# Averages of squares as a 128 by 112 block in a hybrid vision network on one core

## The chip, the cores and the metric

The kernel runs on one core of a Trainium2 chip. The metric is the device time of one execution in microseconds; lower is better. The time before is the median of three runs.

## The reference

Four layers work on an image batch of 4 x 56 x 56 pixels with 96 channels, in fp32. Layer 0 is a vision state-space block: normalization over channels, a projection, four selective scans over the 3136 pixels of an image (rows, rows reversed, columns, columns reversed) with 192 channels and 16 states each, a gated output projection, and a feed-forward part. Layer 1 is another block of that kind with a convolution branch; its scan output is normalized over 192 channels, and its fused output over 96. Layers 2 and 3 are linear attention (no softmax) and a feed-forward part with 8-bit and 16-bit rounding, each behind a normalization.

What the change touches is the normalization, which occurs all over the network:

```python
def _ln(x, g, b, eps=1e-05):
    m = x.mean(-1, keepdims=True)
    v = x.var(-1, keepdims=True)
    return (x - m) * jax.lax.rsqrt(v + eps) * g + b

def _ln_t(v, eps=1e-5):
    m = jnp.mean(v, axis=-1, keepdims=True)
    s = jnp.var(v, axis=-1, keepdims=True)
    return (v - m) / jnp.sqrt(s + eps)
```

## The kernel before, in words

Channels lie on partitions, pixels along the free dimension. An image's 3136 pixels are cut into 7 chunks of 448 (`CW`, `CS`), and a chunk into four blocks of 112 (`NT`).

**The scans.** 2 layers x 4 images x 4 directions x 7 chunks x 2 halves of the channels x 4 groups of states make 1792 rounds. In each round VectorE forms two products of 448 columns (L719) and runs three scans (L726), ScalarE forms three decays (L678) straight into PSUM banks, GpSimd forms the third product (L714) and the multiplication by C (L768), and TensorE spreads B over partitions (L616, bank `b`) and sums over the states into `y` (L799): four products with 32-column weights, each into its own 32 output partitions. Chunk by chunk TensorE also forms the parameters of later chunks (L448, L496).

**The fillers.** All other work on images is put between these steps as "lanes": Python generators that run in chunks (`load`, `middle`, `branch`, `fuse`, `attend`). The order on TensorE, ScalarE, VectorE and GpSimd is the order in which the program issues instructions. Each `yield` of a generator names the slot in which its next step may be issued (C or F, two slots a round), the number of PSUM banks that it will hold, and its declared cost on ScalarE (a) and TensorE (p). In the scans at most 3 chunks are alive (`DEPTH`) and 2 banks are held (`BANKS`); `room` and `spend` keep the declared backlogs below 4.0 and 7.0. The zeros: at most rounds `keep_busy` (L778) issues products with a weight of zeros ahead of the next spread of B, so that TensorE stays busy. Their number is a constant less 1.6 for each unit of p declared since the last time:

```python
self.add_zeros(int(max(0.0, WARM - self.work) + 0.5))   # WARM = 6.8
self.work += PER_P * pe                                 # PER_P = 1.6, in spend
```

**The tail.** When the last scan has ended, `late` widens the limits: 6 chunks alive, 4 banks held, and a ring of all eight PSUM banks (`self.ring`). What is left of `fuse` and `attend` of the last image then runs without the planner's limits on declared costs.

**The normalization.** `factor` (L820) centres a chunk on TensorE, `squares` (L836) squares it on ScalarE, and `spread_factor` (L841) averages the squares over channels, takes the power -0.5, and gives a factor for each pixel and channel by which VectorE multiplies (L889, L1211, L1251; `fuse` first copies the factor of its 192 channels at L1197). `spread_factor` has three ways:

- at the start, before the scans (`self.tables` is false): products with the squares as weights and one column of averages as moving side give a block of 112 pixels by 4; ScalarE adds eps (L864), GpSimd takes the power (L865), and four products spread it (L875);
- in the scans: the same block of 112 by 4 (L860), then Ln and Exp on ScalarE (L870, L871), and four products whose weights are a repeated column of `rs` and whose moving side is the identity (L875);
- in the tail (`self.ring`): one product of the 96 by 96 averages with the squares gives 96 by 448 (L850), and Ln and Exp (L852, L853) on that whole block write over the squares, so nothing has to be spread.

Of the kernel before, what the change touches and what calls it, by code (L numbers as in the profile page):

```python
# [11 lines left out]
F32 = mybir.dt.float32  # L12
# [3 lines left out]
AF = mybir.ActivationFunctionType  # L16
ALU = mybir.AluOpType
# [5 lines left out]
C = 96  # L23
# [5 lines left out]
NT = 112  # L29
CW = 448  # L30
# [137 lines left out]
class Net:  # L168
# [672 lines left out]
    def spread_factor(self, eps, *terms):  # L841

        nc = self.nc
        if self.ring:
            ps, f = self.ps()[:C, :CW], terms[0][0][:C]
            for n, (sq, avg) in enumerate(terms):
                nc.tensor.matmul(ps, avg, sq, start=n == 0, stop=n == len(terms) - 1)  # L850
            yield "F1 a1.2"
            nc.scalar.activation(f, ps, AF.Ln, bias=self.eps[eps][:C])  # L852
            nc.scalar.activation(f, f, AF.Exp, scale=-0.5)  # L853
            yield "C0"
            return f
        ps = self.ps()
        blocks = [slice(q * NT, (q + 1) * NT) for q in range(4)]
        for q, b in enumerate(blocks):
            for n, (sq, avg) in enumerate(terms):
                nc.tensor.matmul(ps[:NT, q : q + 1], sq[:, b], avg[:, :1], start=n == 0, stop=n == len(terms) - 1)  # L860
        rs = self.wp.tile([NT, 4], F32, name="rs", bufs=12)
        if not self.tables:
            yield "F0 a.3"
            nc.scalar.activation(rs, ps[:NT, :4], AF.Identity, bias=self.eps[eps][:NT])  # L864
            nc.gpsimd.tensor_tensor(rs, rs, self.power[:NT], ALU.pow)  # L865
            yield "C1 p2.4"
        else:

            yield "F1 a.6"
            nc.scalar.activation(rs, ps[:NT, :4], AF.Ln, bias=self.eps[eps][:NT])  # L870
            nc.scalar.activation(rs, rs, AF.Exp, scale=-0.5)  # L871
            yield "C1 p2.4"
        ps = self.ps()[:C, :CW]
        for q, b in enumerate(blocks):
            nc.tensor.matmul(  # L875
                ps[:, b], rs[:, q : q + 1].to_broadcast([NT, C]), self.ident[:NT, :NT], start=True, stop=True
            )
        return ps
# [553 lines left out]
```

## Time and profile before

| | |
|---|---|
| median of three runs | 8124.83 us (8120.56 to 8125.09) |
| the profiled execution, its own time | 8113.91 us |
| its span, first to last instruction | 8112.0 us |
| mean granted TensorE clock | 0.898 of full speed |
| start, before the scans run steadily | to about 122 us |
| scans with fillers | about 122 to 7897 us |
| tail | about 7897 to 8112 us |
| calls of `spread_factor`: start, scans, tail | 5, 213, 34 |

How to read it: PE is TensorE, PEld its weight loads, DVE VectorE, ACT ScalarE, POOL GpSimd, SP the engine that issues the DMAs here. A line of a group or list names the source line, the engine, the operation and the tiles (out<-in). In a list of waits, "DVE h L719 <- PE b L616" means that VectorE's L719 waited until TensorE's L616 was done, followed by the total in us, the times, and the longest. An fp32 matmul counts as two instructions. Busy ends of TensorE are modelled, so distances between starts say more than durations.

### The profile page before, as it was taken

To read this page: it belongs to the slowest core of one execution; us is meant where nothing else is said; L and a number is where in the kernel's file an instruction comes from. 1 tells how busy PE (TensorE), PEld (TensorE's weight loads), DVE (VectorE), ACT (ScalarE), POOL (GpSimd) and SP (SyncE) were. 2 spreads that over 40 slices of the span, in tenths; PEclk is the share of its full clock that TensorE was granted. 3 is DMA by queue.
4 is the path that set the end of the run, shared out by engine and by line. 5 is a ranking of instruction groups with operands and counts; after the bars stand their busy time and mean duration, and the time that the engine had idled before them with its cause. 6 is when DMAs were issued, how large, how long until landed. Compare 5 with 4: busy or idle time off the path is not lost.

```text
span 8112.0 us, 112271 instructions
## 1 busy us (share of the span) xinstructions
PE 7168.4 (88%) x33189; PEld 2503.7 (31%) x33189; DVE 7522.7 (93%) x9600; ACT 6094.8 (75%) x12759; POOL 7167.9 (88%) x3989
## 2 busy tenths in 40 slices
PE   7889888889888988889889889998899988999887
PEld 3233233222332223322232223333233322433233
DVE  6999999999999999999999999999989999899982
ACT  6778878786778767886677866787767877678776
POOL 5999999999999999999989998899988999789980
PEclk8889989899998988999889998889988898898987
DMA  5555665567556666566555665555655556555552
GB/s 177 180 185 188 198 193 183 174 198 222 182 179 193 208 196 188 178 201 193 189 180 180 197 220 176 174 162 169 195 178 164 168 174 195 167 164 166 173 163 66
DMA packets 568235, 1467.46 MB, mean 181 GB/s; under 512 B 108034, under 2 KB 337156, under 8 KB 566756
## 3 DMA queue, kind: packets, MB, share of 16 engines
q1 hardware_dynamic: 566848, 1458.49, 57.3%
q8 instruction: 261, 4.28, 0.2%
q14 instruction: 354, 2.90, 0.1%
q10 hardware_dynamic: 772, 1.80, 0.1%
HBM read 1186.49 MB, written 273.47 MB: 180 GB/s over the span
## 4 chain that ended last, share of the span: by engine, by line
PE 34%; DVE 30%; ACT 16%; issue 12%; POOL 4%; DMA 2%; SPq 0%; DVEq 0%; POOLq 0%; ACTq 0%
DVE h L726 22%; PE y L799 7%; DVE h L719 7%; PE y L786 5%; ACT da L678 5%; PE y L795 4%; PE b L616 3%; POOL hc L768 2%; PE pp L496 2%; ACT L830 2%; PE pp L448 2%; PE ps L875 1%; PE ps L947 1%; PE ps L860 1%; ACT Y L806 1%
## 5 line engine op out<-in xcount | busy, mean ns | idle before, releaser
L726 DVE TENSOR_TENSOR_SCAN h<-da,h 128x449 f32<-128x449 f32 (+1 forms) x5376 | 5505.1, 1071 | 101.0 <-ACT da L678 84.0
L768 POOL TENSOR_TENSOR hc<-h,cb 128x1344 f32<-128x1344 f32 x1792 | 4883.1, 2725 | 615.1 <-DVE h L726 490.0
L678 ACT ACTIVATE da<-dt,na 128x448 f32<-128x448 f32 x5376 | 3353.6, 632 | 1109.4 <-DVE h L726 1087.3
L719 DVE TENSOR_TENSOR h<-du,b 128x448 f32<-128x448 f32 x3584 | 2015.8, 603 | 132.5 <-PE b L616 86.3
L799 PE MATMUL y<-hc,four 128*32 128x448 f32 x14336 | 1918.2, 610 | 18.8 <-POOL hc L768 18.5
L714 POOL TENSOR_TENSOR h<-du,cb 128x448 f32<-128x448 f32 x1792 | 1753.5, 979 | 54.4 <-ACT h L691 29.8
L786 PE MATMUL y<-w,zeros 128*96 128x448 bf16 x5067 | 1415.0, 398 | 0.0
L616 PE MATMUL b<-cf,sel 128*128 128x448 bf16 x1792 | 679.1, 379 | 667.5 <-DVE h L719 661.1
L786 PEld LDWEIGHTS <-zeros 128*96 128x96 bf16 x5067 | 629.3, 135 | 1168.5 <-issue 1011.7
L448 PE MATMUL pp<-U,wd 96*128 96x448 f32 x896 | 666.6, 833 | 14.2 <-DMA U<-u 4.5
L799 PEld LDWEIGHTS y<-hc,four 128*32 128x32 f32 x14336 | 294.8, 113 | 1198.6 <-issue 681.3
L795 PE MATMUL y<-Y,ident 96*96 96x448 f32 x672 | 542.1, 896 | 37.8 <-ACT Y L806 19.8
L496 PE MATMUL pp<-cf,wd 12*96 12x448 f32 (+1 forms) x896 | 484.8, 623 | 89.9 <-ACT dtc L506 55.8
L521 POOL TENSOR_TENSOR duc<-dtc,U 96x896 f32<-96x896 f32 x224 | 482.9, 2156 | 34.6 <-ACT dtc L508 34.6
L696 ACT COPY carry<-h 128x3 f32<-128x3 f32 x1536 | 302.0, 197 | 260.6 <-DVE h L726 254.6
L806 ACT COPY Y<-y 96x448 f32<-96x448 f32 x448 | 342.1, 764 | 29.7 <-PE y L799 28.5
L691 ACT COPY h<-carry 128x3 f32<-128x3 f32 x1536 | 280.0, 182 | 51.3 <-POOL hc L768 48.4
L587 ACT COPY cf<-pp 64x448 f32<-64x448 f32 x448 | 235.6, 526 | 81.0 <-PE pp L609 72.7
L506 ACT ACTIVATE dtc<-pp,wd 96x448 f32<-96x448 f32 x448 | 281.6, 629 | 18.5 <-PE pp L496 14.0
L616 PEld LDWEIGHTS <-sel 128*128 128x128 bf16 x1792 | 184.9, 103 | 349.2 <-issue 280.7
L860 PEld LDWEIGHTS ps<-avg,w 96*112 96x112 f32 (+2 forms) x1936 | 246.2, 191 | 94.7 <-issue 58.4
L875 PEld LDWEIGHTS ps<-ident,rs 112*96 112x96 f32 x1744 | 217.3, 187 | 131.4 <-issue 89.4
(381 smaller groups left out, 5597.3 us busy)
## 6 DMA issues: line engine op xcount, KB each, us to landing
cb<-cd SPq DMA_DIRECT2D x896, 448.0 KB, 4.8
dt<-dd SPq DMA_DIRECT2D x448, 672.0 KB, 5.6
du<-dd SPq DMA_DIRECT2D x448, 672.0 KB, 5.8
dd<-dtc SPq DMA_DIRECT2D x672, 112.0 KB, 2.0
dd<-duc SPq DMA_DIRECT2D x672, 112.0 KB, 2.0
win<-m SPq DMA_DIRECT2D x252, 112.0 KB, 4.4
U<-u SPq DMA_DIRECT2D x112, 168.0 KB, 4.6
w<-z SPq DMA_DIRECT2D x84, 224.0 KB, 4.3
```

What stands on the lines that cost most here:

```text
L448: self.nc.tensor.matmul(ch.ps.rearrange("p (a b) -> p a b", b=HS), ch.par.wx[:, e], self.in_order(self.U[e], ch.orient, ch.c * CS, CS), st ...
L496: self.nc.tensor.matmul(ch.pd, ch.par.wt[rows, C * e : C * e + C], ch.cf[rows], start=True, stop=True)
L521: self.nc.gpsimd.tensor_tensor(in_rows(ch.duc), in_rows(ch.dtc), u[:, :, lo : lo + CS // HS], ALU.mult)
L616: self.nc.tensor.matmul(ps, self.sel[:, q], self.upper(ch.cf), start=True, stop=True)
L678: nc.scalar.activation(da[g][:, INNER], ch.dt[e][:, g], AF.Exp, scale=ch.par.na[:, e, q, g : g + 1])
L714: nc.gpsimd.tensor_tensor(tokens(hs[n])[:, 2], ch.du[e][:, 2], ch.cb[q][:, 1], ALU.mult)
L719: nc.vector.tensor_tensor(tokens(hs[n])[:, g], ch.du[e][:, g], bs[n], ALU.mult)
L726: nc.vector.tensor_tensor_scan(h[:, way], da[g][:, way], h[:, way], 0.0, ALU.mult, ALU.add)
L768: nc.gpsimd.tensor_tensor(hc, tokens(hs[n]), ch.cb[q][:, 0].unsqueeze(1).to_broadcast([128, NG, CS]), ALU.mult,)
L786: self.nc.tensor.matmul(self.y[:C], self.zeros[:, :C], self.some, start=False, stop=False)
L795: nc.tensor.matmul(o, w, self.in_order(a, ch.orient, ch.c * CS, CS), start=True, stop=False)
L799: nc.tensor.matmul(self.y[32 * n : 32 * n + 32], self.four, hc[:, g], start=n == 3, stop=n == 3 or q == NQ - 1,)
```

## The change

In the scans and in the tail, `spread_factor` averages the squares by four products with 32 columns of averages as weights (`avg[:, :32]`) and a block of 112 pixels as the moving side. Each product writes its own 32 partitions, so the result is a block of 128 partitions by 112, in which each 32 partitions repeat one block's averages. For two terms (in `fuse`) the four products of the second term follow those of the first. Ln and Exp act on this 128 by 112 block into a new tile `rsb` with 4 buffers. Four more products spread it: the weights are an identity column (0, 32, 64 or 96) repeated over 96 columns, the moving side is `rsb`. The declared cost of this last step is p1.4, where the old spread declared p2.4. The tail loses its own way: its factor now lies in a PSUM bank, and the step after Exp holds a bank and goes through TensorE. The way of the start stays, with 3 buffers of `rs` in place of 12.

```diff
         nc = self.nc
-        if self.ring:
-            ps, f = self.ps()[:C, :CW], terms[0][0][:C]
-            for n, (sq, avg) in enumerate(terms):
-                nc.tensor.matmul(ps, avg, sq, start=n == 0, stop=n == len(terms) - 1)
-            yield "F1 a1.2"
-            nc.scalar.activation(f, ps, AF.Ln, bias=self.eps[eps][:C])
-            nc.scalar.activation(f, f, AF.Exp, scale=-0.5)
-            yield "C0"
-            return f
         ps = self.ps()
         blocks = [slice(q * NT, (q + 1) * NT) for q in range(4)]
+        if self.tables:
+            for n, (sq, avg) in enumerate(terms):
+                for q, b in enumerate(blocks):
+                    nc.tensor.matmul(
+                        ps[32 * q : 32 * q + 32, :NT], avg[:, :32], sq[:, b], start=n == 0, stop=n == len(terms) - 1
+                    )
+            rs = self.wp.tile([128, NT], F32, name="rsb", bufs=4)
+            yield "F1 a.6"
+            nc.scalar.activation(rs, ps[:, :NT], AF.Ln, bias=self.eps[eps])
+            nc.scalar.activation(rs, rs, AF.Exp, scale=-0.5)
+            yield "C1 p1.4"
+            ps = self.ps()[:C, :CW]
+            for q, b in enumerate(blocks):
+                row = self.ident[:, 32 * q : 32 * q + 1].to_broadcast([128, C])
+                nc.tensor.matmul(ps[:, b], row, rs, start=True, stop=True)
+            return ps
         for q, b in enumerate(blocks):
             for n, (sq, avg) in enumerate(terms):
                 nc.tensor.matmul(ps[:NT, q : q + 1], sq[:, b], avg[:, :1], start=n == 0, stop=n == len(terms) - 1)
-        rs = self.wp.tile([NT, 4], F32, name="rs", bufs=12)
-        if not self.tables:
-            yield "F0 a.3"
-            nc.scalar.activation(rs, ps[:NT, :4], AF.Identity, bias=self.eps[eps][:NT])
-            nc.gpsimd.tensor_tensor(rs, rs, self.power[:NT], ALU.pow)
-            yield "C1 p2.4"
-        else:
-
-            yield "F1 a.6"
-            nc.scalar.activation(rs, ps[:NT, :4], AF.Ln, bias=self.eps[eps][:NT])
-            nc.scalar.activation(rs, rs, AF.Exp, scale=-0.5)
-            yield "C1 p2.4"
+        rs = self.wp.tile([NT, 4], F32, name="rs", bufs=3)
+        yield "F0 a.3"
+        nc.scalar.activation(rs, ps[:NT, :4], AF.Identity, bias=self.eps[eps][:NT])
+        nc.gpsimd.tensor_tensor(rs, rs, self.power[:NT], ALU.pow)
+        yield "C1 p2.4"
         ps = self.ps()[:C, :CW]
         for q, b in enumerate(blocks):
             nc.tensor.matmul(
```

## The prediction

> **What bounds the kernel now.** I read the page from the top: span and engine shares, then VectorE's and TensorE's lists of waits inside the scan stage (122 to 7897 us, some 96% of the span), then one averaging step in the timeline of TensorE, then the busy time in stretches of the tail.
>
> The engine shares (busy us, share of the span, instructions) come first.
>
> ```profile
> span 8112.0 us, 112271 instructions
> PE   7168.4 (88%) x33189; PEld 2503.7 (31%) x33189; DVE 7522.7 (93%) x9600; ACT 6094.8 (75%) x12759; POOL 7167.9 (88%) x3989
> ```
>
> VectorE is the busiest. From 122 to 7897 us it works 7410.4 of 7775 us, so only 365 us (4.7%) of the scan stage are open to any gain at all, unless VectorE's own work shrinks, and the change doesn't shrink it. What ends its idle time there (us in total, times, longest):
>
> ```profile
> DVE h L726 <- ACT da L678: 81.4, 165, 2.5
> DVE h L719 <- PE b L616: 76.7, 93, 2.9
> DVE w L889 <- PE ps L875: 33.5, 19, 3.7
> ...
> DVE xra L889 <- PE ps L875: 10.3, 10, 2.7
> ...
> DVE xq L1251 <- PE ps L875: 7.3, 4, 4.2
> ...
> DVE w L1211 <- PE ps L875: 3.6, 4, 2.0
> ```
>
> Two kinds of TensorE lateness touch the change: the spread of B (L616) comes late 93 times in 1792 rounds, and the spread factor (L875) 37 times, 54.7 us together. TensorE itself mostly waits for VectorE:
>
> ```profile
> PE b L616 <- DVE h L719: 654.1, 713, 2.8
> ```
>
> So TensorE has slack in most rounds and is late in a few crowded ones. An averaging step, as TensorE runs it (start, duration, instructions):
>
> ```profile
> 4011.96 0.86 PE L860 MATMUL ps<-avg,w 96*112 96x1 f32 x8
> 4012.68 0.36 PE L616 MATMUL b<-cf,sel 128*128 128x448 bf16 x1
> 4012.97 0.96 PE L799 MATMUL y<-hc,four 128*32 128x448 f32 x8
> 4013.85 1.02 PE L448 MATMUL pp<-U,wd 96*128 96x448 f32 x2
> 4014.71 0.92 PE L824 MATMUL ps<-w,cen 96*96 96x448 f32 x2
> 4015.46 0.93 PE L875 MATMUL ps<-ident,rs 112*96 112x112 f32 x8
> 4016.23 0.36 PE L616 MATMUL b<-cf,sel 128*128 128x448 bf16 x1
> ```
>
> Starts are the better measure, since ends are modelled. The average (L860) takes 4012.68 - 4011.96 = 0.72 us, the spread (L875) 4016.23 - 4015.46 = 0.77 us, a full 448-column product (L824) 0.75 us. Each fp32 product is two instructions.
>
> The tail (us of the stretch; then busy PE, weight load, DVE, ACT, POOL, clock, DMA):
>
> ```profile
> 7900.00:7945.00 45.00, 42.45 (x128) 14.08 (x127) 9.44 (x16) 24.88 (x48) 5.37 (x4) 0.96 0.34 83
> 7974.00:8020.00 46.00, 37.59 (x120) 16.27 (x119) 18.16 (x36) 41.48 (x86) 5.14 (x5) 0.85 0.12 34
> 8058.00:8090.00 32.00, 23.71 (x73) 9.46 (x72) 13.69 (x28) 29.54 (x62) 4.11 (x4) 0.79 0.08 22
> ```
>
> TensorE fills the first stretch, ScalarE the other two; between them (7945 to 7974, 8020 to 8058) neither does, and a chain of short steps sets the time.
>
> [...]Ln took 263 ns on 4 columns (L870) and 629 on 448 (L852), 0.82 ns each; Exp 206 (L871) and 577 (L853). [...]The eight of L860 follow one another at 0.72 / 8 = 90 ns[...]. [...]The sums y (L799), four 32-column products side by side, took 4013.85 - 4012.97 = 0.88 us where two full instructions take 0.75[...].
>
> **The change part by part.** Calls of the averaging helper: 218 on the block path (1744 / 8), of which 5 in the start use the power path (L864) and stay as they are; 213 in the scans; 34 in the tail (L853). L860's 1936 / 8 = 242 terms are the 218 calls and 24 second terms of calls from fuse. Without the start: 189 single and 24 double calls in the scans, and 30 single and 4 double in the tail.
>
> Average, new form: eight instructions of 112 columns per term. L875's are of that length at 0.77 / 8 = 0.096 us each. Bounds: 0.19 us if four run wholly side by side[...], 0.77 if they don't overlap at all. By y I take 2 x 0.096 + 0.13 = 0.32 for one term and 0.51 for two. Scans: 0.72 - 0.32 = 0.40 saved on each of 189, 1.44 - 0.51 = 0.93 on each of 24: 98 us of TensorE.
>
> Spread, new form: still four products of 112 columns with 96-column weights, 0.77 us; the weights are now constant and only the moving side waits for Exp. I count nothing for that.
>
> Zeros: keep_busy pads TensorE up to 6.8 zero products less 1.6 per declared unit. The spread is declared at 1.4 in place of 2.4, which allows 1.6 more zeros per call. Seven zeros took 4047.13 - 4045.71 = 1.42 us, 0.20 each, so at most 213 x 1.6 x 0.20 = 68 us; where q is 0, or other work already fills the budget, none come. I take two thirds, 45 us. They stand directly ahead of L616, so b waits behind them, and VectorE's products wait for b. TensorE's balance in the scans is 98 - 45 = 53 us less.
>
> ScalarE, scans: Ln and Exp on 112 columns instead of 4 cost 0.09 more each, 213 x 0.18 = 38 us. Against it, Ln waits less for its average (56.1 us in 54 waits now; 0.4 each would be 22 us). ScalarE is at 76% there. Behind Ln and Exp in its queue stand the decays (L678), which VectorE's scan awaits.
>
> What reaches the end in the scans: 130 stalls (93 + 37) of about 1 us. A crowded stretch with one averaging call loses 0.40 us from the average and gains about 0.2 from zeros. If two thirds of the stalls contain a call: 130 x 0.67 x 0.2 = 17 us. ScalarE gives back 213 x 0.18 x 9% (165 of 1792 rounds are late on L678), 3 us. Sum: 14 us less.
>
> Tail: Ln and Exp fall from 629 + 577 to about 352 + 295 ns, 0.56 us less a call, 19 us of ScalarE. TensorE gains work: single calls -0.75 + 0.32 + 0.77 = +0.34, double calls -1.50 + 0.51 + 0.77 = -0.22; 30 x 0.34 - 4 x 0.22 = +9 us. Calls by stretch are 6, 7, 10, 5, 5 and 1. In the two ScalarE stretches 15 calls free 8.4 us, but TensorE rises by 5 and is at 82% and 74%, so I credit 5. In the first stretch TensorE gains 1 us at most. In the chains, average, Ln and Exp took 0.75 + 0.64 + 0.58 and will take 0.32 + 0.35 + 0.30 + 0.77, with one more hand-over: I call it 1 us less over 12 calls. The result now holds a bank from the spread to the multiplication, and a TensorE instruction waits for Exp where only VectorE did: other chunks' centring and FFN products queue behind it. From -5 to +15 us; I take -1. Tail: 6 us less.
>
> Free edits: rs with 3 buffers serves only the start, where at most 3 chunks are alive; rsb with 4 matches that depth and the tail's 4 banks. No DMA and no POOL instruction is added, so SP's queue is untouched. The lower declared cost also lets the planner admit fillers earlier, but two banks held at once limit it before its TensorE limit of 7.0 does (two steps make at most 2.4 + 3.9), so I expect nearly the same order and count nothing, with 10 us either way for the range.
>
> Sum: 14 + 6 = 20 us. The profiled execution took 8113.91 us, 11 below the median of 8124.83; I apply the difference to the median: 8105.
>
> **The rivals.**
> (a) TensorE relieved, as above: 8105 (own range 8075 to 8118). Chance 0.40; it counts as faster.
> (b) The relief falls where TensorE waits for VectorE anyway (713 waits), and the tail trades ScalarE for TensorE one to one: 8125. Chance 0.26. The 4.7% of idle VectorE time speaks for it.
> (c) Slower: the extra zeros delay b. Place: between the fillers of one round and L616 of the next. Price: up to 68 us if the average gives nothing back in the same rounds; half of that on VectorE's path gives 8125 + 34, about 8159. It decides once TensorE enters those rounds over some 3 us late, since b is due only after three scans (3.05 us); only 93 rounds are there now, which speaks against it. For it: L616 is already the largest TensorE wait, and the planner believes the new spread is a whole unit cheaper though its columns are the same. Chance 0.34, with the tail's longer bank holds as a smaller addition.
> (d) The four products don't run side by side (0.77 us a term): no relief in the scans, and 38 x 0.45 = 17 us more TensorE in the tail. y speaks against it. About 8140, counted within (c).
>
> **How the numbers follow.** 8105 is (a). The range reaches down to 8065 (TensorE's whole 53 us arriving) and up to 8168 ((c) with some tail loss). A difference under 0.2% (16 us) is about what a measurement of this kernel can't tell from none. Faster 0.40, same 0.26, slower 0.34.
>
> **What would show it.** Right: the average's line at about 0.32 us between starts with four groups overlapping; Ln and Exp near 350 and 295 ns; zeros up by 200 to 340; VectorE's wait for b below 77 us; the tail (from the last scan at about 7897 to the end, 215 us) shorter by about 6. Wrong: an average that takes over 0.5 us, VectorE's wait for b above 77 us, or a tail with TensorE busier and longer than 215 us.

## The result, and the profile after

The changed kernel takes 8015.68 us in the median (8012.27 to 8022.15, four runs), against 8122.69 us before, in four runs too. The ratio is 0.9872, with a 95% interval from 0.9855 to 0.9889: 1.3% faster, some 105 us, where 20 us were forecast. Repeated later on the chip that ran the last experiments, the changed kernel took 8019.67 us against 8119.09, a ratio of 0.9881 (0.9865 to 0.9896).

The span and the engine shares of the changed kernel:

```profile
span 8014.9 us, 113446 instructions
PE 7013.7 (88%) x33765; PEld 2326.8 (29%) x33765; DVE 7522.8 (94%) x9600; ACT 6114.5 (76%) x12759; POOL 7170.8 (89%) x3989
```

VectorE's work is the same to a tenth of a microsecond; what went is its idle time. The last scan now ends at 7810.4 us instead of 7901.3, so the scan stage gave 91 us and the tail (210.7 before, 204.6 after) gave 6. VectorE's waits in the scan stage of the changed kernel, 122 to 7810 us (total, times, longest):

```profile
DVE h L726 <- ACT da L678: 80.0, 173, 1.9
DVE h L719 <- PE b L616: 52.6, 71, 2.8
DVE w L889 <- PE ps L863: 28.8, 18, 3.5
...
DVE w L1203 <- PE ps L1201: 9.9, 9, 2.2
...
DVE xra L889 <- PE ps L863: 5.2, 9, 0.8
```

The wait for b fell from 76.7 to 52.6 us. The new spread factor (L863) comes late for 36 us in all its lines, where L875 made 55. But the wait for L1201 (at L1203) also fell, from 26.7 to 9.9 us, and L1201 is a product in `fuse` which the change doesn't touch: the gain reaches work that only stands near the averages.

**Where.** Set side by side round by round, the two traces show where the time went. Most of the gain, 65 of 91 us, lies in the first 56 rounds of the last three images of layer 1, in which `fuse` of the image before runs as a filler, and 11 us more in the last 56 rounds of all, where `fuse` of the last image begins. Of the other stretches of 56 rounds none gave 5 us. The three stretches, about 3% of the rounds each, in the kernel before (the stretch, its length; then busy PE, weight load, DVE, ACT, POOL; TensorE's clock, DMA share, GB/s):

```profile
4889.00:5164.00 275.00, 261.27 (x1260) 110.81 (x1258) 246.72 (x322) 181.69 (x423) 224.83 (x126) 0.88 0.56 176
5884.00:6160.00 276.00, 262.16 (x1255) 109.39 (x1255) 246.25 (x321) 181.52 (x422) 224.25 (x126) 0.88 0.55 174
6878.00:7163.00 285.00, 271.49 (x1257) 115.54 (x1255) 246.81 (x321) 181.20 (x422) 224.37 (x126) 0.84 0.53 169
```

and the same rounds in the changed kernel:

```profile
4886.00:5140.00 254.00, 231.91 (x1260) 83.72 (x1260) 244.65 (x321) 184.26 (x421) 224.43 (x126) 0.94 0.59 188
5859.00:6117.00 258.00, 234.97 (x1261) 85.22 (x1260) 245.99 (x322) 184.67 (x422) 224.82 (x127) 0.93 0.58 186
6829.00:7086.00 257.00, 234.61 (x1260) 85.24 (x1260) 245.03 (x320) 183.97 (x420) 223.83 (x126) 0.93 0.58 185
```

Read the rows in this order. TensorE was busy for 95% of these stretches before, VectorE for 87 to 90%: here, unlike in the rest of the stage, TensorE was the bound. After, VectorE is at 95 to 96% and TensorE at 91%. And the clock column moved: 0.84 to 0.88 before, 0.93 to 0.94 after. The page of before showed 0.898 for the whole run, which hid that these full stretches ran at a lower clock.

The average itself, in TensorE's timeline of the changed kernel (L852, one term and then two):

```profile
4940.73 0.40 PE L852 MATMUL ps<-w,avg 96*32 96x112 f32 x8
4941.06 0.79 PE L786 MATMUL y<-w,zeros 128*96 128x448 bf16 x3
...
4954.10 0.72 PE L852 MATMUL ps<-w,avg 128*32 128x112 f32 x16
4954.76 0.59 PE L786 MATMUL y<-w,zeros 128*96 128x448 bf16 x2
```

By the distance between starts it takes 0.33 us for one term and 0.66 for two, in these lines as in the median. The old two-term average, in the kernel before:

```profile
4966.41 2.34 PE L860 MATMUL ps<-avg,w 128*112 128x1 f32 x16
4968.68 0.60 PE L786 MATMUL y<-w,zeros 128*96 128x448 bf16 x2
```

It took 2.27 us, not twice 0.72. (For one term 0.72 us is the least; the median is 0.81.) Inside it, two weight loads of equal rows start 0.095 us apart, but from a 128-row load to a 64-row one and back it is about 0.19: each of eight changes of the row count costs some 0.1 us.

### The profile page after: what moved, and what is told of

The parts are those of the page before. It is cut to its first block, busy times and chain, and to the rows that moved or that the text cites. A ratio compares the mean times of both kernels' runs of the same rounds, so it can differ in the third digit from the quotient of the medians.

```text
span 8014.9 us, 113446 instructions
## 1 busy us (share of the span) xinstructions
PE 7013.7 (88%) x33765; PEld 2326.8 (29%) x33765; DVE 7522.8 (94%) x9600; ACT 6114.5 (76%) x12759; POOL 7170.8 (89%) x3989
## 4 chain that ended last, share of the span: by engine, by line
DVE 32%; PE 31%; ACT 17%; issue 13%; POOL 4%; DMA 2%; DVEq 0%; SPq 0%; POOLq 0%; ACTq 0%
DVE h L726 23%; DVE h L719 7%; PE y L799 6%; ACT da L678 5%; PE y L786 5%; PE y L795 4%; PE b L616 3%; POOL hc L768 2%; PE pp L496 2%; ACT L830 2%; PE ps L947 2%; PE pp L448 1%; ACT Y L806 1%; PE ps L863 1%; PE ps L824 1%
## 5 line engine op out<-in xcount | busy, mean ns | idle before, releaser
L786 PE MATMUL y<-w,zeros 128*96 128x448 bf16 x5143 | 1433.0, 397 | 0.0
L496 PEld LDWEIGHTS pp<-cf,wd 12*96 12x96 f32 (+1 forms) x896 | 113.6, 165 | 468.5 <-ACT dtc L506 175.6
L863 PEld LDWEIGHTS ps<-rsb,ident 128*96 128x96 f32 x1768 | 207.3, 178 | 126.3 <-issue 77.6
```

The lines of the kernel that those rows point to most:

```text
L496: self.nc.tensor.matmul(ch.pd, ch.par.wt[rows, C * e : C * e + C], ch.cf[rows], start=True, stop=True)
L786: self.nc.tensor.matmul(self.y[:C], self.zeros[:, :C], self.some, start=False, stop=False)
```

## The experiments

Three theories were to be told apart. **A**: TensorE's time in the averages, saved where TensorE is full. **B**: the planner's order and zeros, which changed with the declared 1.4 units. **C**: the clock: in the old averages TensorE mostly loads weights and has one moving column a product (in the stretches before, L860's weight loads are busy for 86.0 us and its products for 89.1; in those after, L852's for 14.2 and 31.5), the clock is halved after that, and everything on TensorE is slower. Products with many moving columns are called streaming here. "Stretches" below are the three from above, with their summed length and mean clock in the profiled execution; before they have 834.8 us and 0.87, after 769.6 and 0.93. Ratios are to runs of the kernel before on the same chip (medians of 8110 to 8119 us); where a gain is given in us beside a ratio, it is worked out from the ratio. Code is shortened where "..." stands.

**1. The new operations in the old order** (`e_after_p24`, from the changed kernel):

```diff
-            yield "C1 p1.4"
+            yield "C1 p2.4"
```

> The changed kernel with the spread declared at 2.4 units as before, so that the planner issues nearly the old order and the old number of zero products, but every operation is the new one. Theory A (TensorE's work in the stretches of fuse, where TensorE is full): most of the 105 us stay, about 8030 us. Theory B (the planner's order and zeros under the lower declared cost made the gain): most of it goes, about 8100 us.

Measured: 8036.81 us, ratio 0.9903 (0.9889 to 0.9917); zeros 5067, as before; stretches 776 us, clock 0.93. Most of the gain stays without the new order.

**2. The old operations in the new order** (`e_before_p14`, from the kernel before, in the way of the scans):

```diff
-            yield "C1 p2.4"
+            yield "C1 p1.4"
```

> The kernel before with one number changed: the spread in the scans declared at 1.4 units in place of 2.4. All operations are the old ones; order and number of zeros are the planner's for the lower cost. Theory A: no gain, 8122 us or some 10 us more for the zeros. Theory B: most of the 105 us, about 8035 us.

Measured: 8102.53 us, ratio 0.9993 (0.9983 to 1.0003); zeros 5143, as in the changed kernel; stretches 842 us, clock 0.87. B falls as the main cause. The order did change, at 225 of VectorE's some 9600 places, but alone it moves nothing. Together with the new operations it may give another 0.2 to 0.3%: 0.9903 against 0.9872 and 0.9881, with intervals that touch.

**3. A wider moving side** (`e_wide`, from the kernel before):

```diff
-                nc.tensor.matmul(ps[:NT, q : q + 1], sq[:, b], avg[:, :1], start=n == 0, stop=n == len(terms) - 1)
+                o = ps[:NT, 32 * q : 32 * q + 32] if self.tables else ps[:NT, q : q + 1]
+                w = avg[:, : o.shape[1]]
+                nc.tensor.matmul(o, sq[:, b], w, start=n == 0, stop=n == len(terms) - 1)
...
-            nc.scalar.activation(rs, ps[:NT, :4], AF.Ln, bias=self.eps[eps][:NT])
+            one = ps[:NT, :128].rearrange("p (q c) -> p q c", c=32)[:, :, 0]
+            nc.scalar.activation(rs, one, AF.Ln, bias=self.eps[eps][:NT])
```

> The kernel before, with the moving side of the old average 32 columns wide in place of 1 in the scans (the other 31 columns are equal and unused; Ln reads every 32nd). TensorE's time per average should stay at 0.72 us[...]. Theory C ([...]the changed kernel gains by the clock): clock in the stretches of fuse from 0.87 towards 0.93, 25 to 50 us faster, about 8085 us. Theory A without C: 8122 us, same clock.

Measured: 8116.93 us, ratio 1.0008 (1.0000 to 1.0016); stretches 843 us, clock 0.87. As it stands this spoke against C, and I went on with A. The clock didn't move either, so the run says nothing about what a better clock would bring; with 96 columns in place of 32 it was 0.96 to 0.97 (run 9).

**4. No alternation of rows** (`e_rows`, from the kernel before): the second squares of `fuse` are made 128 rows high by weights padded with zero columns.

```diff
-            pb = self.ps()[:64, :CW]
-            nc.tensor.matmul(pb, self.neg192[:, :64], ya, start=True, stop=False)
-            nc.tensor.matmul(pb, self.cen192[:64, :64], yb, start=False, stop=True)
+            pb = self.ps()[:, :CW]
+            nc.tensor.matmul(pb, self.half_neg, ya, start=True, stop=False)
+            nc.tensor.matmul(pb, self.half_cen[:64], yb, start=False, stop=True)
...
-            f = yield from self.spread_factor(1e-5, (sa, self.avg192), (yb, self.avg192[:64]))
+            f = yield from self.spread_factor(1e-5, (sa, self.avg192), (ya, self.avg192))
```

> The kernel before, with the second squares of fuse made 128 rows high (64 rows of zeros) so that the two-term old average no longer alternates between products of 128 and of 64 rows; all else is as before. If the alternation costs 8 times 0.1 us, the 16 instructions take about 1.45 us in place of 2.27, and with TensorE full in those stretches 24 x 0.8 = 19 us come off: about 8103 us. If the 2.27 us have another cause, 8122 us and no shorter average.

Measured: 8067.81 us, ratio 0.9944 (0.9928 to 0.9960), some 45 us; the 16 instructions take 1.59 us, 0.68 less. Stretches 805 us, clock 0.89. The alternation is shown as a cost, but 24 x 0.68 = 16 us of TensorE brought nearly three times as much: something multiplies. The clock records of this run offer the rest: TensorE's time at half speed in the stretches fell from 222 to 171 us, and half of the difference is 26 us.

**5 and 6. Two-term averages alone, one-term averages alone** (`e_double`, `e_single`, from the kernel before): the new way under a condition, behind the tail's own branch, so that the tail stays as it was in both runs; the two expectations have this wrong. Of the 24 two-term calls in the scans 21 lie in the stretches.

```diff
+        if self.tables and len(terms) == 2:      # e_double; == 1 in e_single
+            ...the new way...
```

> The kernel before, with the new way for fuse's two-term averages alone (28 calls, 24 of them in the scans); all one-term averages and the tail's own way stay old. Two-term averages fall from 2.27 to 0.63 us. If gain equals TensorE time saved where TensorE is full: 24 x 1.64 = 39 us, ratio 0.995. If saved time is amplified, as in the run that took away the alternation (45 us for 24 x 0.68 = 16 us): 70 us or more, ratio 0.991. If the one-term averages matter as much as the two-term ones: under 30 us.

Measured: 8045.96 us, ratio 0.9936 (0.9922 to 0.9949), some 52 us; stretches 777 us, clock 0.93.

> The complement: the new way for all one-term averages, in scans and tail; fuse's two-term averages stay old. One-term averages fall from 0.81 to 0.33 us, some 50 of them lie in the stretches where TensorE is full: 50 x 0.48 = 24 us there, and about 6 from the tail, ratio 0.996. If the two-term averages carried nearly all: ratio 0.999.

Measured: 8086.74 us, ratio 0.9969 (0.9962 to 0.9976), some 25 us; stretches 830 us, clock 0.87. So 24 calls in the scans bring about 52 us, and the 189 one-term calls of the scans half of that. In the stretches alone the two-term calls do nearly everything: 777 us is within 8 of the changed kernel, and the clock comes with them.

**7. The old tail** (`e_scans`, from the kernel before): the new way for both kinds of averages, again behind the tail's own branch, which is kept.

```diff
+        if self.tables and not self.ring:
+            ...the new way...
```

> The changed kernel in the scans, the old way (whole 96 by 448 block, no spread) in the tail. If the gain lies in the scans: ratio 0.988 and a tail of about 211 us, as before. If the tail gave more than the 6 us that the two profiles show: ratio 0.990 or above.

Measured: 8030.22 us, ratio 0.9908 (0.9893 to 0.9923), some 75 us, about the sum of runs 5 and 6; tail 212.8 us, stretches 767 us. Most of the gain lies in the scans. The ratio is on the side that I had expected if the tail gave more than 6 us, but the profiles don't bear that out: the tail is 8 us longer than in the changed kernel, and the last scan ends 12 us later (7822.9 against 7810.4), though the stretches are as short. Where those 12 us come from stays open; the intervals of the two ratios just meet.

**8. The saved time given back as streaming** (`e_pad`, from the changed kernel):

```diff
+            for again in range(1 if self.ring else 3 if len(terms) == 1 else 5):
             for n, (sq, avg) in enumerate(terms):
                 ...the four products...
```

> The changed kernel, where in the scans the new average's products are repeated, three times for one term and five times for two, so that an average takes about as long on TensorE as the old one (0.33 + 2 x 0.19 = 0.71 us, 0.63 + 4 x 0.37 = 2.1 us)[...]. If TensorE's time alone made the gain: nearly all of it goes, ratio 0.998 to 1.0. If the halved clock that follows the old averages made a large part: about half of the gain stays, ratio 0.993, and a clock of at least 0.92 in the stretches of fuse.

Measured: 8020.98 us, ratio 0.9905 (0.9891 to 0.9918). An average now takes 0.71 us for one term and 3.28 for two, against 0.81 and 2.27 in the kernel before. Still some 77 us of about 100 are there by the ratio, and in the profile the last scan ends within 1 us of the changed kernel's. The first of the stretches in this kernel:

```profile
4873.00:5131.00 258.00, 241.88 (x1921) 93.64 (x1923) 245.38 (x321) 183.60 (x421) 225.55 (x127) 0.99 0.59 187
```

A alone falls here: the stretches take 775 us together, 5 more than in the changed kernel, though 21 x 2.6 = 55 us of products were added there to the two-term averages alone. The clock is 0.99, and TensorE is busy for only 7 to 10 us more in each stretch. VectorE, busy for 245 of 258 us, is near its limit in both.

**9. The old average, 96 columns wide** (`e_wide96`, from the kernel before):

```diff
-                nc.tensor.matmul(ps[:NT, q : q + 1], sq[:, b], avg[:, :1], start=n == 0, stop=n == len(terms) - 1)
+                o = ps[:NT, 96 * q : 96 * q + 96] if self.tables else ps[:NT, q : q + 1]
+                w = avg[:, : o.shape[1]]
+                nc.tensor.matmul(o, sq[:, b], w, start=n == 0, stop=n == len(terms) - 1)
...
+            one = ps[:NT, :384].rearrange("p (q c) -> p q c", c=96)[:, :, 0]
+            nc.scalar.activation(rs, one, AF.Ln, bias=self.eps[eps][:NT])
```

> The kernel before, with the moving side of the old average 96 columns wide in the scans (95 of them equal and unread). The weight loads stay and set at least 0.72 us for one term and 2.27 for two, so TensorE's time doesn't fall[...]. Theory C (what counts is that the array streams, so that the clock isn't halved): clock in the stretches of fuse above 0.92, 40 us or more faster, ratio 0.995 or below. Theory A (TensorE's time in those averages): ratio 1.000.

Measured: 8033.32 us, ratio 0.9893 (0.9877 to 0.9908). Its two-term average and its second stretch:

```profile
4913.23 2.98 PE L862 MATMUL ps<-avg,w 128*112 128x96 f32 x16
4916.14 0.97 PE L1190 MATMUL ps<-w,neg 128*64 128x448 f32 x2
```

```profile
5860.00:6118.00 258.00, 242.74 (x1255) 101.46 (x1255) 245.33 (x322) 180.69 (x422) 224.15 (x126) 0.97 0.59 186
```

This is the plainest of the runs. Order, zeros, weight loads, alternation and the old way of spreading are all those of the kernel before. Each average takes longer on TensorE than it did (4916.14 - 4913.23 = 2.91 us against 2.27). Only the moving side is wider, 96 columns in place of 1, the clock rises from 0.88 to 0.97 in this stretch, and 86 us come off. C holds.

The clock record of the kernel before shows the same link piece by piece. It consists of pieces of 3.4 us at full or at half speed, and the three stretches have 180 pieces at full speed. In 12 of these at least 12 of the 16 instructions of a two-term average began, and half speed followed all 12, though TensorE shows no more than 0.02 us of idle time in any of them. In 111 no instruction with one moving column began, and half speed followed 6. Of the 57 with fewer such instructions it followed 15.

**10. The old average put back** (`e_after_loads`, from the changed kernel): the old two-term average is issued as well, unread, in the scans.

```diff
+            if len(terms) == 2 and not self.ring:
+                for q, b in enumerate(blocks):
+                    for n, (sq, avg) in enumerate(terms):
+                        nc.tensor.matmul(ps[:NT, 256 + q : 257 + q], sq[:, b], avg[:, :1], start=n == 0, stop=n == 1)
```

> The changed kernel, with the old two-term average issued as well ahead of the new one in the scans (its result unread): 16 products of 1 column on 112-column weights, alternating rows, 2.27 us each time. Padding with streaming products of 2.6 us cost some 5 us in all. Theory C: this padding costs far more, the clock in the stretches of fuse falls below 0.90, 40 us or more slower than the changed kernel (above 8055 us). Theory A with slack to spare: the same 5 to 10 us as the streaming padding, about 8025 us.

Measured: 8100.22 us, ratio 0.9978 (0.9971 to 0.9985), 80 us slower than the changed kernel beside it. Its second stretch:

```profile
5880.00:6157.00 277.00, 261.07 (x1372) 103.74 (x1372) 245.79 (x321) 183.71 (x421) 224.14 (x126) 0.88 0.55 172
```

In the three stretches 21 x 2.27 = 48 us of work were added, and they grew by 65 us, to 834; in run 8, 55 us of streaming work made them 5 us longer. The clock is back at 0.88, the length at 277 us.

**11. Streaming behind the old average** (`e_before_stream`, from the kernel before): three unread sets of the new two-term products after each old two-term average.

```diff
+        for again in range(3 if self.tables and len(terms) == 2 else 0):
+            for n, (sq, avg) in enumerate(terms):
+                for q, b in enumerate(blocks):
+                    nc.tensor.matmul(ps[32 * q : 32 * q + 32, 128 : 128 + NT], avg[:, :32], sq[:, b], start=n == 0, stop=n == 1)
```

> The kernel before, with work added: behind each two-term old average in the scans, three unread sets of the new two-term products, about 1.3 us of streaming on TensorE where it is full. Theory C: faster in spite of it, clock in the stretches of fuse above 0.90, ratio 0.995 to 0.998. Theory A: slower by 24 x 1.3 = 31 us, ratio 1.004.

Measured: 8187.41 us, ratio 1.0089 (1.0072 to 1.0105), some 72 us slower than before; clock 0.80 to 0.86. My expectation from C was wrong here, and A's 31 us were too few as well. The streaming work added here didn't make up for the old average beside it. One place in the timeline (the old average, the added products, then products of `fuse`), and the second stretch:

```profile
4902.33 2.34 PE L860 MATMUL ps<-avg,w 128*112 128x1 f32 x16
4904.61 2.04 PE L864 MATMUL ps<-w,avg 128*32 128x112 f32 x48
4906.57 1.70 PE L1191 MATMUL ps<-w,neg 128*64 128x448 f32 x2
```

```profile
5913.00:6209.00 296.00, 282.09 (x1591) 117.77 (x1591) 247.00 (x321) 181.20 (x421) 224.20 (x126) 0.86 0.51 161
```

The added products take 1.96 us here, not the 1.3 that I had expected, and up to 3.19 us elsewhere. The clock record puts half speed from 4906.7 us on, right behind them: L1191 takes 1.64 us between starts where it takes 0.90 elsewhere. By the count of run 9, half speed followed all 17 pieces that hold most of a two-term average. The time at half speed in the stretches rose from 222 to 297 us; (297 - 222) / 2 = 37 us and 21 x 1.96 = 41 us of added work together are about the 74 us by which the stretches grew. Why the time at half speed rose, and didn't merely stay, is open.

**12. The changed kernel again** (`after_again`), as the measure for runs 9 to 11:

> The changed kernel unaltered, on the chip of the three other runs, as their measure. Earlier it took 8015.68 us; I expect 8010 to 8025 us and a ratio of 0.988.

Measured: 8019.67 us, as given above. No version here beats it. The padded and the wide one come within 7 us of its length in the stretches, where VectorE is busy for 245 of 258 us.

## Why the prediction was wrong, point by point

- **The sign was right, and so was it that the gain lies in crowded rounds of the scans; the size was off by five times** (20 us against 105). The step that failed is "What reaches the end in the scans", with 14 us in place of 91, in two ways: it took VectorE for the bound everywhere, and it held TensorE's clock constant.
- **The bound.** That step began from VectorE's list of waits over the whole stage: 130 stalls of about 1 us, each to be shortened by 0.2 us. In three stretches of about 275 us TensorE was the bound (busy 795 of 836 us), and 96 us of VectorE's 365 idle us lay there. Most of them were no stalls of the kind that the step counted: VectorE waited 56 us there for other products and squares of `fuse` (L1203, L1185 and L1192). A table of stretches, which I made for the tail only, would have shown it. TensorE's busy time in the stretches fell by 93 us, VectorE's idle time to 33 us, and the length by 65 us, against 14 forecast for the whole stage.
- **The clock.** This is the larger omission. By the clock records TensorE ran at half speed for 222 us of the three stretches before, 106 us after, 48 us with 96 columns and 14 us with streaming padding. The records hold only 1.0 and 0.5, nearly all in pieces of 3.4 us and its multiples. If half a microsecond of work is lost in each of these microseconds, as the 0.5 suggests (in run 11 L1191 took 1.64 us there and 0.90 elsewhere), that makes (222 - 106) / 2 = 58 us, an estimate. Idle time of TensorE was not what went ahead of it there: TensorE idled for only 14 us of each stretch of 275 to 285, and not at all in 11 of the 12 pieces counted at run 9 (0.02 us in the other). What went with it was the old two-term average: the clock was 0.96 to 0.97 when its moving side had 96 columns (run 9), and 0.88 again when it was put back beside the new one (run 10).
- **The old averages were mis-sized**: 2.27 us for two terms, not 1.44, because 128 and 64 rows alternate (run 4), and 0.81 us in the median for one, not 0.72, which one place in the timeline had shown. To the new form I had added 0.13 us, what y's 0.88 us exceed 0.75 by (an estimate), and I had not looked for such a cost in the old one, where each change of the row count takes some 0.1 us; whether the two have one cause, no run shows. The new average was right for one term (0.32 forecast, 0.33 measured) and too short for two (0.51 against 0.66). So 189 x 0.48 + 24 x 1.61 = 129 us of TensorE went, not 98.
- **Zeros**: 76 more, not 200 to 340, about 15 us rather than 45; why so few, no run shows. In runs 1 and 2 they follow the declared cost and move little. Rival (c) rested on them and fell: the wait for b shrank.
- **"Nearly the same order"** holds for VectorE's sequence (225 of some 9600 places differ in run 2), and the order alone moved nothing; what it adds beside the new operations stays open at 0.2 to 0.3%.
- **The spread** cost the same as before (0.84 us in the median in both), as counted. **Ln and Exp** took 348 and 297 ns (352 and 295 forecast).
- **The tail** lost 6 us, as forecast, but in part by luck. ScalarE lost 14 us, not 19, TensorE gained 3, not 9, and TensorE's clock rose from 0.80 to 0.86, which the forecast did not have. From the last scan to the end, before and after:

```profile
7901.00:8112.00 211.00, 164.88 (x523) 68.61 (x519) 58.96 (x121) 141.51 (x280) 22.66 (x20) 0.80 0.25 66
7810.00:8015.00 205.00, 167.61 (x1027) 89.94 (x1019) 60.25 (x121) 127.08 (x280) 22.66 (x20) 0.86 0.23 68
```

- **Rivals**: (b) and (d) fell too: the relief did not vanish in TensorE's idle time, and the four products do run side by side: they take 0.33 us together, against the 0.77 that (d) counted.

What stays open: how few columns or what share of streaming keep the clock up (0.87 with 32, 0.96 to 0.97 with 96, on 112-column weights), why streaming right beside an old average didn't help (run 11), and how the 45 us of run 4 divide: 16 us less work and 26 us of half speed would nearly explain them, but no run separates the two. Nor is it settled how the changed kernel's own gain divides between less work on TensorE and the better clock: run 9 has 86 us of the 99 without any saving of work in the averages, and with the better clock VectorE is near its limit (245 of 258 us busy), so that the two don't add up.

## What to carry to other kernels

Read the profile by stretches before summing anything: a stage that is bound by one engine on average can have a few per cent of its time in which another is full (here TensorE, busy for 795 of 836 us), and there a saving counts until the next engine is full (here VectorE, busy for 736 of 769 us after). On TensorE, ask not only how long a product takes but how much of it streams: here, products with one moving column on 112-column weights were paid twice, once as time (2.27 us for two terms) and once as a halved clock for what followed (half speed after all 12 pieces that hold most of such an average). Try the larger operand as the moving side (here 0.33 and 0.66 us in place of 0.81 and 2.27), and look for products of different row counts that alternate (here some 0.1 us a change).

## What the runs showed of the hardware that was not expected

- Adding work to TensorE made the kernel faster: 96 moving columns in place of 1 took 2.91 us in place of 2.27 for two terms, and the kernel came down from 8119 to 8033 us.
- An old two-term average of 2.27 us added to the changed kernel, result unread, cost 80 us over 24 calls, 3.4 us for each, while 2.6 us of streaming added to each made the three stretches 5 us longer in all.
- A change between 128-row and 64-row products cost about 0.1 us each time; without them 16 instructions took 1.59 us in place of 2.27.
- Half speed followed all 12 pieces of 3.4 us that held most of an old two-term average, though TensorE shows no more than 0.02 us of idle time in any of them.
- Streaming right behind an old average didn't hold the clock: 0.80 to 0.86 in run 11, 0.84 to 0.88 before.
